# Seven products with fewer additions: M1 seeded in PSUM, M5 put where C22 will be

## The chip, the cores and the metric

The kernel runs on one core of a Trainium2 chip. Its time is the device time of that core in microseconds; three runs of the kernel before took 2271.55 to 2274.96 us, median 2273.53 us. The engines are TensorE (PE, with its weight loads as PEld), VectorE (DVE), ScalarE (ACT), GpSimd (POOL) and SyncE (SP), which issues most of the transfers.

## The reference

There are 32 graphs of 512 nodes with 512 features each, `x` and `adj` of shape (32, 512, 512), all fp32. Two layers follow each other, each with a residual:

```python
# layer 0
h = maximum(layernorm(x), 0)
deg = sum(adj, -1)
agg = (adj @ h) / maximum(deg, 1e-6)
x = x + relu(concat([h, agg], 2) @ W.T)          # W: (512, 1024)
# layer 1
h = maximum(layernorm(x), 0)
q, k = split(h @ Wqk, 2);  v = h @ Wv            # Wqk: (512, 1024), Wv: (512, 512)
agg = adj @ (k * mask)
w = mask * sum(q * agg, -1) / sqrt(512)
x = x + softmax(w, over the nodes)[..., None] * v
```

## The kernel before

**What is multiplied.** With A = adj divided by its row sums, W1 and W2 the halves of W, and M = Wq Wkᵀ, the kernel computes for each graph Y = h W2ᵀ and O = h W1ᵀ + A Y (layer 0), then U = A (mask h1), T = h1 M and V = h1 Wv (layer 1). The score of a node is the sum over a row of T times U.

**How each product is made.** A 512x512 by 512x512 product is done as 2x2 blocks of 256x256 with seven block products M1 to M7 in place of eight, which costs sums of blocks before and after. The operands' sums lie in seven slots of a tile (`left_sums`, `right_sums`, L102 to L113; `LEFT` and `RIGHT` say which slot belongs to which M). The results are

```
C11 = M1 + M2          C12 = M1 + M6 + M5 + M3
C21 = M1+M6+M7 + M4    C22 = M1+M6+M7 + M5
```

`product` (L118) does this for Y, O and U, and for V of the last graph. Its inner `m` issues one M: for each pair of operands four matmul calls, in the profile 8 rows of 128x256, into one bank of PSUM (128 x 512 fp32). Y and U have one pair of operands, O has two (h with W1, A with Y), so an M of O is twice as long. The bank `pp` collects M1, then M6, M7 and M4 on top (`start` is False), `pq` collects M5 and M3, `pr` holds M2. Between them ScalarE copies what has to be kept (`copy`, L100) and `finish` lets VectorE add (`add`, L94). A matmul that writes on into a bank waits until the engine that reads the bank is done. Before M6 this is ScalarE's copy of M1, before M7 its copy of M1+M6, before M3 its copy of M5, before M4 its copy of M1+M6+M7.

T and V together (`layer1_tv`, `ptv` in the profile) are two levels deep: seven outer M, each of seven inner block products, spread over four banks; the four parts of a bank set are added by VectorE (tv<-ptv). The inner results are put together later by `recombine` (tv<-tv). The last graph, and T and V of the one before it, use `layer1_one` (`pw`), one of T and V at a time.

**The order of work.** Four phases follow each other for each graph, written out by hand: O of graph i (14 steps), T and V of graph i−1 (14 steps), U of graph i (7 steps), Y of graph i+1 (7 steps). `run` (L167) takes a phase, which yields once per step, and a `Plan`, which says what else is queued after the matmuls of each step: statistics, sums, transposes, loads and stores of other graphs. A step's order in the queues is: its matmuls, then the plan's work of that step, then the copies and adds with which `product` finishes the step. Each engine works through its queue in the order of the program (`manual_schedule`); there is no planner.

In U the plan gives VectorE `turn` of h1T (four transposes), `recombine` (seven), `dot` (four multiplications with a sum, L611), `scores`; in Y `turn` of aT (two transposes, L278), `row_sum`, `sums` of A, `weights` and seven more `recombine`.

**Buffers.** All PSUM tiles come from one pool of eight banks. `block` (L87) gives SBUF tiles of 128 x 512 from a ring of four; O uses it for C11, C12, C22 and M5, Y and U for M5 alone, since their C lie in the result's own tile (`into`, L420). The tiles of h and A in `start` come from the same ring. W1 in its seven slots is loaded again for each graph by `Stream`, in the order `ORDER`, in which O takes them.

Of the kernel before, what the change touches and what calls it, by code (L numbers as in the profile page):

```python
# [11 lines left out]
F32 = mybir.dt.float32  # L12
# [4 lines left out]
P = 128  # L17
# [5 lines left out]
def kernel(  # L23
# [32 lines left out]

    nc = tc.nc
    B, N, F = x.shape  # L60
    C = N // P
    H = F // 2
# [6 lines left out]
    big = ctx.enter_context(tc.tile_pool(name="big", bufs=1))  # L69
    small = ctx.enter_context(tc.tile_pool(name="small", bufs=2))  # L70
    dram = ctx.enter_context(tc.tile_pool(name="dram", bufs=2, space=bass.MemoryType.DRAM))
    ps_m = ctx.enter_context(tc.tile_pool(name="ps_m", bufs=8, space=bass.MemoryType.PSUM))


    LEFT = {1: 0, 2: 1, 3: 2, 4: 3, 5: 4, 6: 5, 7: 6}
# [3 lines left out]

    PLACE = {2: 0, 3: 1, 4: 2, 7: 3, 1: 4, 6: 5, 5: 6}  # L80
    AT = {p: j for j, p in PLACE.items()}
    ORDER = [1, 2, 6, 5, 7, 3, 4]

    def slots(tag, bufs, name, pool=None):
        return (pool or big).tile([P, 7, 2, H], F32, tag=tag, bufs=bufs, name=name)

    def block(name):  # L87
        return big.tile([P, 2, H], F32, tag="tmp", bufs=4, name=name)

    def mm_tile(name):  # L90
        return ps_m.tile([P, 2, H], F32, tag="m", name=name)

    def add(o, a, b, on=None):
        (on or nc.vector).tensor_tensor(o, a, b, op=ALU.add)  # L94
# [4 lines left out]
    def copy(o, i):  # L99
        nc.scalar.activation(o, i, AF.Copy)  # L100
# [14 lines left out]
    def of(t):  # L115
        return lambda i: t[:, i]

    def product(name, terms, place, finish):  # L118

        def m(k, p, first):
            n = 0
            for lt, rt in terms:
                right = rt(k)
                for rc in range(2):
                    for dk in range(2):
                        nc.tensor.matmul(  # L130
                            p[:, rc, :],
                            lt[:, LEFT[k], dk, ts(rc, P)],
                            right[:, dk, :],
                            start=first and n == 0,
                            stop=True,
                            skip_group_check=True,
                        )
                        n += 1
                yield

        pp = mm_tile(f"pp_{name}")
        yield from m(1, pp, True)
        c11 = place(0, 0)
        copy(c11, pp)
        pr = mm_tile(f"pr_{name}")
        yield from m(2, pr, True)
        finish(0, 0, c11, pr, c11)
        yield from m(6, pp, False)
        c12 = place(0, 1)
        copy(c12, pp)  # L150
        pq = mm_tile(f"pq_{name}")
        yield from m(5, pq, True)
        m5 = block(f"m5_{name}")
        copy(m5, pq)
        yield from m(7, pp, False)
        c22 = place(1, 1)
        copy(c22, pp)
        finish(1, 1, c22, m5, c22)
        yield from m(3, pq, False)
        finish(0, 1, c12, pq, c12)  # L160
        yield from m(4, pp, False)
        finish(1, 0, None, pp, None)

    def right(t):
        return lambda k: t[:, RIGHT[k]]
# [264 lines left out]

    def layer0_y(b):
        y = Y[b] = slots("yh", 1, f"y_{b}")
        return product(f"y_{b}", [(hT, right(w2R))], *into(y))

    def layer0_out(b, w1):
        def place(r, c):
# [14 lines left out]
    def layer1_tv(b):  # L451

        t = TV[b] = tv
        left = H1T[b]

        def m(k, banks, first):
            for half in ((2, 1), (3, 0)):
                for n in half:  # L460
                    if first:
                        banks[n] = mm_tile(f"ptv_{b}_{k}_{n}")
                    for i, p in enumerate(range(2 * n, min(2 * n + 2, 7))):
                        j = AT[p]
                        nc.tensor.matmul(  # L465
                            banks[n][:, :, ts(i, P)],
                            left[:, LEFT[k], LEFT_IN[j], :],
                            mvR[:, RIGHT[k], RIGHT[j], :, :],
                            start=first and i == 0,
                            stop=True,  # L470
                            skip_group_check=True,
                        )
                yield half

        def part(o, n):
            first = [0, 4, 8, 10][n] + (2 if n < 2 else 3) * (o % 2)
            return t[:, o // 2, :, first:first + min(2, 7 - 2 * n), :].rearrange("p w b f -> p w (b f)")

        def parts(k, banks, first, use):
            for half in m(k, banks, first):  # L480
                yield
                for n in half:
                    use(n, banks[n][:, :, 0:P * min(2, 7 - 2 * n)])

        def keep(o):
            return lambda n, p: copy(part(o, n), p)

        def plus(o):
            return lambda n, p: add(part(o, n), p, part(o, n))

        pp, pr, pq, m5 = {}, {}, {}, {}

        def keep5(n, p):
            m5[n] = block(f"m5_tv_{b}_{n}")[:, :, 0:P * min(2, 7 - 2 * n)]
            copy(m5[n], p)

        yield from parts(1, pp, True, keep(0))
        yield from parts(2, pr, True, plus(0))
        yield from parts(6, pp, False, keep(1))
        yield from parts(5, pq, True, keep5)  # L500
        yield from parts(7, pp, False, lambda n, p: add(part(3, n), p, m5[n]))
        yield from parts(3, pq, False, plus(1))
        yield from parts(4, pp, False, keep(2))

    def layer1_one(b, which, held=None):

        t = TV[b] = tv
        left = H1T[b]

        def m(k, banks, first):  # L510
            for n in range(2):
                if first:
                    banks[n] = mm_tile(f"pw_{which}_{b}_{k}_{n}").rearrange("p a f -> p (a f)")
                for i, p in enumerate(range(4 * n, min(4 * n + 4, 7))):
                    j = AT[p]
                    s = LEFT[k]
                    nc.tensor.matmul(  # L517
                        banks[n][:, ts(i, P)],
                        held[:, s, :] if held is not None and j == 3 else left[:, s, LEFT_IN[j], :],
                        mvR[:, RIGHT[k], RIGHT[j], which, :],  # L520
                        start=first and i == 0,
                        stop=True,
                        skip_group_check=True,
                    )
                yield n

        def part(o, n):
            rows = t[:, o // 2, which]
            if n == 0:
                return rows[:, 0:8, :].rearrange("p (n c i) f -> p n c i f", n=2, c=2)[:, :, o % 2]  # L530
            return rows[:, 8 + 3 * (o % 2):11 + 3 * (o % 2), :]

        def like(n, p):
            if n == 0:
                return p.rearrange("p (n i f) -> p n i f", n=2, i=2)
            return p[:, 0:3 * P].rearrange("p (i f) -> p i f", f=P)

        def parts(k, banks, first, use):
            for n in m(k, banks, first):
                yield  # L540
                use(n, like(n, banks[n]))

        def keep(o):
            return lambda n, p: copy(part(o, n), p)

        def plus(o):
            return lambda n, p: add(part(o, n), p, part(o, n))

        pp, pr, pq, m5 = {}, {}, {}, {}

        def keep5(n, p):
            m5[n] = like(n, block(f"m5_w_{which}_{b}_{n}").rearrange("p a f -> p (a f)"))
            copy(m5[n], p)

        yield from parts(1, pp, True, keep(0))
        yield from parts(2, pr, True, plus(0))
        yield from parts(6, pp, False, keep(1))
        yield from parts(5, pq, True, keep5)
        yield from parts(7, pp, False, lambda n, p: add(part(3, n), p, m5[n]))
        yield from parts(3, pq, False, plus(1))  # L560
        yield from parts(4, pp, False, keep(2))

# [16 lines left out]
    class Post:  # L579
# [71 lines left out]
        def finish(self, r, c):  # L651

            v = self.blocks[r, c]
            for a in range(2):
                o = self.o[:, 2 * r + a, ts(c, H)]
                nc.vector.scalar_tensor_tensor(
                    o, v[:, a, :], self.sm[:, 2 * r + a:2 * r + a + 1], o, op0=ALU.mult, op1=ALU.add
                )
# [88 lines left out]
    def start():  # L747
# [42 lines left out]
            for k in range(2):  # L790
                turn_right(s2[h], h, k, w2R)
        for c in range(C):
            v = block(f"h_{c}").rearrange("p a f -> p (a f)")
            nc.scalar.activation(
                in_order(v), natural(X[0][:, c, :]), AF.Relu, scale=t[1][:, c:c + 1], bias=t[2][:, c:c + 1]
            )
            turn_chunk(v, c, "h")
# [7 lines left out]
        rows = {}  # L805

        def scale_a(c):
            rows[c] = block(f"a_{c}").rearrange("p a f -> p (a f)")
            nc.scalar.activation(
                in_order(rows[c]), natural(fa.n[c // 2][:, c % 2, :]), AF.Copy, scale=fa.rdeg[:, c:c + 1]  # L810
            )
# [395 lines left out]
```

## Time and profile before

| | before |
|---|---|
| median time | 2273.53 us |
| TensorE busy | 2259.1 us, 99% |
| VectorE busy | 1923.6 us, 85%, 3803 instructions |
| ScalarE busy | 1025.6 us, 45%, 1896 instructions |
| GpSimd busy | 174.8 us, 8% |
| granted TensorE clock | 0.999 |

A row of the order of time gives the start and the length of a merged group in us, the engine, the line, the operation with output and inputs by their names in the program, the shape, the number of instructions, and in brackets how long the engine sat idle before it and what ended that. Consecutive instructions on one engine overlap in the records by some 0.08 us on VectorE and 0.16 us on TensorE, so the distance between starts, not the length, is what one costs in a row: 8 matmul rows of an M are 1.89 us long, and the next M starts 1.73 us after. The lines of helpers stand for all their uses: L130 is every matmul of `product`, L94 every addition on VectorE, L97 every subtraction, L100 every ScalarE copy; the names of the tiles tell them apart.

### The profile page before, as it was taken

What the parts mean: (1) busy time and instruction counts of PE and PEld (TensorE: products, weight loads), DVE (VectorE), ACT (ScalarE), POOL (GpSimd) and SP (SyncE); (2) the same over time, 40 slices, a digit from 0 to 9 for tenths busy, and PEclk for the clock granted to TensorE, in tenths of its full rate; (3) what the DMA queues carried; (4) which work ended last, traced back from release to release, by engine and by line L of the source; (5) the groups of instructions that cost most, each with busy time, mean ns of one, the idle gap of its engine ahead of it and who ended that gap; (6) DMA issues with size and microseconds to landing.
All of it is one profiled execution on the core that took longest, in us unless ns stands there. A gap on an engine that the chain in (4) does not pass through costs nothing.

```text
span 2271.4 us, 32927 instructions
## 1 busy us (share of the span) xinstructions
PE 2259.1 (99%) x10550; PEld 1978.7 (87%) x10550; DVE 1923.6 (85%) x3803; ACT 1025.6 (45%) x1896; POOL 174.8 (8%) x260
## 2 busy tenths in 40 slices
PE   9999999999999999999999999999999999999998
PEld 7788888888888888888888888888888888888897
DVE  7798888888888888888888888888888888888778
ACT  4454443445434554444454344544444543445323
POOL 0000010000100000100000000000000010000000
PEclk9999999999999999999999999999999999999999
DMA  9978787887878777777878888777888787878543
GB/s 222 233 214 246 204 212 193 205 230 206 210 199 202 213 220 207 208 191 207 227 210 205 199 201 218 218 207 202 196 210 225 209 209 193 205 219 217 154 123 96
DMA packets 409773, 463.68 MB, mean 204 GB/s; under 512 B 37729, under 2 KB 271713, under 8 KB 405377
## 3 DMA queue, kind: packets, MB, share of 16 engines
q1 hardware_dynamic: 400192, 428.56, 69.5%
q0 software_dynamic: 8928, 32.51, 8.7%
q8 instruction: 83, 1.36, 0.3%
q14 instruction: 90, 0.73, 0.1%
q10 hardware_dynamic: 480, 0.52, 0.1%
HBM read 293.93 MB, written 167.51 MB: 203 GB/s over the span
## 4 chain that ended last, share of the span: by engine, by line
PE 93%; DMA 3%; DVE 2%; SPq 1%; ACT 0%; issue 0%; DVEq 0%; POOLq 0%; ACTq 0%
PE ptv L465 28%; PE pp_o L130 18%; PE pp_u L130 9%; PE pq_o L130 9%; PE pp_y L130 9%; PE pq_u L130 5%; PE pr_o L130 5%; PE pq_y L130 5%; PE pr_u L130 2%; PE pr_y L130 2%; PE pw L517 1%; DMA a<-in_adj_dram 1%; SPq L212 0%; DVE tv L94 0%; DMA room<-in_L_gnn_Wqk_dram 0%; DVE mv L97 0%
## 5 line engine op out<-in xcount | busy, mean ns | idle before, releaser
L465 PE MATMUL ptv<-mv,h1T 128*128 128x256 f32 x2940 | 639.7, 379 | 0.1
L465 PEld LDWEIGHTS ptv<-mv,h1T 128*128 128x128 f32 x2940 | 558.5, 190 | 76.4 <-DVE xu L444 0.5
L94 DVE TENSOR_TENSOR tv<-tv 128x256 f32<-128x256 f32 (+1 forms) x658 | 326.4, 508 | 13.4 <-ACT tv L100 1.5
L100 ACT ACTIVATE tv<-ptv 128x512 f32<-128x512 f32 (+1 forms) x360 | 184.9, 541 | 262.9 <-PE ptv L465 262.0
L130 PE MATMUL pp_y<-wide 128*128 128x256 f32 x1024 | 242.1, 379 | 1.5 <-ACT y L100 1.2
L130 PE MATMUL pp_u<-h1m,aT 128*128 128x256 f32 x1024 | 242.0, 379 | 0.0
L130 PE MATMUL pp_o<-y,aT 128*128 128x256 f32 x1024 | 241.9, 379 | 0.0
L130 PE MATMUL pp_o<-w,wide 128*128 128x256 f32 x992 | 234.3, 379 | 0.0
L130 PEld LDWEIGHTS pp_y<-wide 128*128 128x128 f32 x1024 | 194.2, 190 | 28.5 <-ACT y L100 1.6
L130 PEld LDWEIGHTS pp_u<-h1m,aT 128*128 128x128 f32 x1024 | 194.4, 190 | 27.0 <-issue 0.7
L130 PEld LDWEIGHTS pp_o<-y,aT 128*128 128x128 f32 x1024 | 194.5, 190 | 26.4
L130 PEld LDWEIGHTS pp_o<-w,wide 128*128 128x128 f32 x992 | 188.5, 190 | 25.6
L100 ACT ACTIVATE o<-pp_o 128x512 f32<-128x512 f32 x96 | 57.2, 596 | 296.0 <-PE pp_o L130 296.0
L100 ACT ACTIVATE y<-pp_y 128x512 f32<-128x512 f32 x128 | 76.3, 596 | 234.5 <-PE pp_y L130 233.4
L94 DVE TENSOR_TENSOR tv<-ptv,tv 128x512 f32<-128x512 f32 x240 | 139.6, 613 | 43.7 <-PE ptv L465 38.4
L97 DVE TENSOR_TENSOR h1T<-h1T 128x512 f32<-128x512 f32 (+2 forms) x193 | 165.8, 873 | 1.2
L100 ACT ACTIVATE xu<-pp_u 128x512 f32<-128x512 f32 x128 | 76.4, 597 | 195.9 <-PE pp_u L130 195.9
L246 POOL TENSOR_TENSOR rstd<-rstd,mhalf 128x2 f32<-128x2 f32 (+1 forms) x96 | 78.7, 820 | 651.0 <-DVE rstd L245 651.0
L130 PE MATMUL pq_y<-wide 128*128 128x256 f32 x512 | 121.0, 379 | 0.0
L130 PE MATMUL pq_o<-y,aT 128*128 128x256 f32 x512 | 121.0, 379 | 0.0
L130 PE MATMUL pq_u<-h1m,aT 128*128 128x256 f32 x512 | 121.0, 379 | 0.0
L94 DVE TENSOR_TENSOR tv<-ptv,m_tv 128x512 f32<-128x512 f32 (+1 forms) x120 | 72.0, 622 | 55.6 <-PE ptv L465 55.1
(130 smaller groups left out, 3269.4 us busy)
## 6 DMA issues: line engine op xcount, KB each, us to landing
w<-dw SPq DMA_DIRECT2D x217, 256.0 KB, 4.3
xu<-in_x_dram SPq DMA_DIRECT2D x128, 256.0 KB, 5.3
a<-in_adj_dram SPq DMA_DIRECT2D x256, 128.0 KB, 3.0
dh1T<-h1m SPq DMA_DIRECT2D x128, 256.0 KB, 3.1
dx<-xu SPq DMA_DIRECT2D x32, 1024.0 KB, 5.1
sh1T<-dh1T SPq DMA_DIRECT2D x256, 128.0 KB, 3.3
shT<-dhT SPq DMA_DIRECT2D x248, 128.0 KB, 6.0
daT<-a SPq DMA_DIRECT2D x124, 256.0 KB, 3.0
```

The source lines that it names most:

```text
L94: (on or nc.vector).tensor_tensor(o, a, b, op=ALU.add)
L97: (on or nc.vector).tensor_tensor(o, a, b, op=ALU.subtract)
L100: nc.scalar.activation(o, i, AF.Copy)
L130: nc.tensor.matmul(p[:, rc, :], lt[:, LEFT[k], dk, ts(rc, P)], right[:, dk, :], start=first and n == 0, stop=True, skip_group_check=True,)
L246: nc.gpsimd.tensor_tensor(rstd[:, a:b], rstd[:, a:b], mhalf[:, a:b], op=ALU.pow)
L465: nc.tensor.matmul(banks[n][:, :, ts(i, P)], left[:, LEFT[k], LEFT_IN[j], :], mvR[:, RIGHT[k], RIGHT[j], :, :], start=first and i == 0, st ...
L517: nc.tensor.matmul(banks[n][:, ts(i, P)], held[:, s, :] if held is not None and j == 3 else left[:, s, LEFT_IN[j], :], mvR[:, RIGHT[k], RI ...
```

## The change

The order of the block products in `product` becomes M1, M5, M6, M2, M7, M3, M4, and fewer of the additions after them are left to VectorE.

- ScalarE copies M1 from `pp` into another bank of PSUM, `pr`, and M2's matmuls then accumulate there (no `start`), so that C11 = M1 + M2 is finished by TensorE. ScalarE copies it out (Y, U), or the last operation of O reads it in PSUM. A bank of its own (`ps_r`) is kept for this; the seven others stay in the pool. The first Y does it without the seed (`seed=b > 0`), and M2 and M5 of T and V use that bank for the part that fills it.
- M5 is copied by ScalarE to the place of C22, and VectorE adds M1+M6+M7 to it from `pp`. Before, ScalarE copied M1+M6+M7 to C22 as well, and VectorE added the tile of M5.
- In T and V M5 likewise goes to its part of `tv`, and VectorE adds the rest from PSUM.
- The ring of `block` has two tiles in place of four; h and A of the first graph use `tv`, which is free then.

It is for fewer instructions on VectorE and for less SBUF. The diff, cut to its core (`layer1_one` has the same edit as `layer1_tv`):

```diff
-    ps_m = ctx.enter_context(tc.tile_pool(name="ps_m", bufs=8, space=bass.MemoryType.PSUM))
+    ps_m = ctx.enter_context(tc.tile_pool(name="ps_m", bufs=7, space=bass.MemoryType.PSUM))
+    ps_r = ctx.enter_context(tc.tile_pool(name="ps_r", bufs=1, space=bass.MemoryType.PSUM))
...
-    ORDER = [1, 2, 6, 5, 7, 3, 4]
+    ORDER = [1, 5, 6, 2, 7, 3, 4]
...
-        return big.tile([P, 2, H], F32, tag="tmp", bufs=4, name=name)
+        return big.tile([P, 2, H], F32, tag="tmp", bufs=2, name=name)
...
+    def seed_tile(name):
+        return ps_r.tile([P, 2, H], F32, tag="r", name=name)
...
-    def product(name, terms, place, finish):
+    def product(name, terms, place, finish, seed=True):
...
         pp = mm_tile(f"pp_{name}")
         yield from m(1, pp, True)
-        c11 = place(0, 0)
+        pr = seed_tile(f"pr_{name}")
+        c11 = pr if seed else place(0, 0)
         copy(c11, pp)
-        pr = mm_tile(f"pr_{name}")
-        yield from m(2, pr, True)
-        finish(0, 0, c11, pr, c11)
+        pq = mm_tile(f"pq_{name}")
+        yield from m(5, pq, True)
+        c22 = place(1, 1)
+        copy(c22, pq)
         yield from m(6, pp, False)
         c12 = place(0, 1)
         copy(c12, pp)
-        pq = mm_tile(f"pq_{name}")
-        yield from m(5, pq, True)
-        m5 = block(f"m5_{name}")
-        copy(m5, pq)
+        yield from m(2, pr, not seed)
+        if seed:
+            finish(0, 0, None, pr, None)
+        else:
+            finish(0, 0, c11, pr, c11)
         yield from m(7, pp, False)
-        c22 = place(1, 1)
-        copy(c22, pp)
-        finish(1, 1, c22, m5, c22)
+        finish(1, 1, c22, pp, c22)
         yield from m(3, pq, False)
         finish(0, 1, c12, pq, c12)
         yield from m(4, pp, False)
...
-        return product(f"y_{b}", [(hT, right(w2R))], *into(y))
+        return product(f"y_{b}", [(hT, right(w2R))], *into(y), seed=b > 0)
...
-                        banks[n] = mm_tile(f"ptv_{b}_{k}_{n}")
+                        banks[n] = (seed_tile if n == 0 and k != 1 else mm_tile)(f"ptv_{b}_{k}_{n}")
...
-        yield from parts(5, pq, True, keep5)
-        yield from parts(7, pp, False, lambda n, p: add(part(3, n), p, m5[n]))
+        yield from parts(5, pq, True, keep(3))
+        yield from parts(7, pp, False, plus(3))
...
-            v = block(f"h_{c}").rearrange("p a f -> p (a f)")
+            v = tv[:, c // 2, 0, 4 * (c % 2):4 * (c % 2) + 4, :].rearrange("p i f -> p (i f)")
...
-            rows[c] = block(f"a_{c}").rearrange("p a f -> p (a f)")
+            rows[c] = tv[:, c // 2, 1, 4 * (c % 2):4 * (c % 2) + 4, :].rearrange("p i f -> p (i f)")
```

## The prediction

> **What bounds the kernel now.** I read the page's busy shares and chain first, then what TensorE waited for, then the busy time of a long stretch, then the order of time around one graph, and last the form-by-form groups for prices.
>
> ```profile
> PE 2259.1 (99%) x10550; PEld 1978.7 (87%) x10550; DVE 1923.6 (85%) x3803; ACT 1025.6 (45%) x1896; POOL 174.8 (8%) x260
> ...
> PE 93%; DMA 3%; DVE 2%; SPq 1%; ACT 0%; issue 0%; DVEq 0%; POOLq 0%; ACTq 0%
> ```
>
> ```profile
> 189.00:1579.00 1390.00, 1390.00 (x6442) 1223.71 (x6441) 1190.64 (x2367) 639.32 (x1183) 109.84 (x160) 1.00 0.80 209
> ```
>
> ```profile
> PE spare L781 <- DVE late L753: 1.5, 1, 1.5
> PE pp_y L130 <- ACT y L100: 1.2, 1, 1.2
> PE pw L517 <- DVE tv L94: 0.8, 1, 0.8
> PE pp_y L130 <- DVE wide L97: 0.3, 1, 0.3
> ```
>
> The chain runs through TensorE. The second fence is twenty graphs of 69.50 us: TensorE (first "busy") is busy in 1390.00 of 1390.00 us. The third is all it ever waits: under 4 us in a run of 2271. The matmuls don't change, so there is almost nothing to win; the question is whether the change puts a wait where there is none. VectorE, 1190.64 of 1390.00 us, comes next.
>
> Graph 15's U, first TensorE, then VectorE:
>
> ```profile
> 1120.74 1.89 PE L130 MATMUL pp_u<-h1m,aT 128*128 128x256 f32 x8
> 1122.47 1.89 PE L130 MATMUL pq_u<-h1m,aT 128*128 128x256 f32 x8
> 1124.19 1.89 PE L130 MATMUL pp_u<-h1m,aT 128*128 128x256 f32 x8
> ```
>
> ```profile
> 1109.27 2.44 DVE L94 TENSOR_TENSOR tv<-ptv,tv 128x512 f32<-128x512 f32 x4
> 1111.62 2.01 DVE L97 TENSOR_TENSOR h1m<-h1m 128x512 f32<-128x512 f32 x3
> ...
> 1120.74 0.68 DVE L94 TENSOR_TENSOR xu<-pr_u,xu 128x512 f32<-128x512 f32 x1
> 1121.34 1.21 DVE L94 TENSOR_TENSOR tv<-tv 128x256 f32<-128x256 f32 x3
> 1122.47 0.69 DVE L611 SCALAR_TENSOR_TENSOR tv<-tv,xu 128x512 f32<-128x512 f32 x1
> ...
> 1124.91 0.69 DVE L94 TENSOR_TENSOR xu<-m_u,xu 128x512 f32<-128x512 f32 x1
> ```
>
> The three TensorE rows are M7, M3 and M4, 1.727 us apart. VectorE's last row is the C22 add of the same product: it starts 0.72 us after M4 has started and ends (1124.91 + 0.69) 1.41 us after. So VectorE runs late here, and today nobody minds: M4 waits only for ScalarE's copy of M1+M6+M7 (1122.67 to 1123.27).
>
> [...] M7 of the second Y waited 1.2 us for ScalarE's read of its bank. [...] the rows above stand in program order, so an add waits for all that is queued ahead. [...] 684 ns for xu<-m_u (both in SBUF), 680 for xu<-pq_u. [...]
>
> ```profile
> 2225.15 0.69 DVE L94 TENSOR_TENSOR tv<-pw,m_w 128x512 f32<-128x512 f32 x1
> ...
> 2225.89 1.83 PE L517 MATMUL pw<-mv,h1T 128*128 128x128 f32 x14 [0.75 <-DVE tv L94]
> ```
>
> The add ends at 2225.84, TensorE goes on 0.05 us later. These 14 take 1.83 us, where 12 elsewhere in the tail take 1.50 and two more 0.22: the restart adds another 0.1 us. M7 of the second Y (89.86 to 91.69, 1.83 instead of 1.73) shows the same 0.1. So a wait costs its end plus 0.15 us.
>
> **The change, part by part.**
>
> *Removed.* One VectorE add per product (c11 += pr), 96 of them over Y, U and O. Back to back such an add takes 0.60 us (1120.74 to 1121.34), 58 us of VectorE in all; none of it is on the path of TensorE by itself. In O also one ScalarE copy (0.60), in Y and U none (five copies before, five after).
>
> *The seed in PSUM.* ScalarE writes M1 into PSUM. No row shows such a write; a copy to SBUF takes 0.60 us[...]. I take 0.60, between the 0.4 of a half-size copy and a doubled 1.2. M6 waits for it 1.73 us after M1 ends, M2 later still; today's copy of M1 has the same 1.73 us (1115.76 to 1116.36, M6 at 1117.29). Even doubled it is hidden: 0.
>
> *Order 1, 5, 6, 2.* M5 needs its sums one place earlier. In U they are made on VectorE by 1109.4, M5 comes at 1115.6; in O the first sum of Y ends at 1140.7, it is needed at 1143.2. 0, but for the first Y: its M5 needs a left sum that ends at 18.86, where M2 ran at 18.01. M6 waited until 20.22 anyhow, so +0.5.
>
> *The smaller rings.* Two blocks serve O, which now needs two. Seven PSUM banks and the seed bank: banks come back in the same order as with eight. Hidden behind the M-stages of 1.7 to 3.5 us: 0.
>
> *C22 by VectorE from PSUM.* This is the part that counts. Four waits of TensorE for a bank (M6, M7, M3, M4) were all on ScalarE; now M4 waits for VectorE's add c22 += pp. Ahead of that add stands everything that the plan gave VectorE up to then. On M4 wait all later matmuls.
>
> - U. VectorE's work is pinned to TensorE at the last of the four tv adds: M3 of T and V gives its last result at 1113.83 − 3.02 + 0.16 = 1110.97, and that add starts at 1111.03. From there VectorE has no gap up to the C22 add. One add (0.60) goes out of this row, the rest stands. The C22 add would end at 1125.60 − 0.60 = 1125.00, M4 goes on as if started at 1125.15, against 1124.19: 0.96 us lost. The next T and V, where VectorE waits for TensorE again (1.48 us at 1105.90), wipes the slate, so it comes again with each graph. I read the same 1.41 in graphs 3 to 29 (1.50 in one), 1.94 in 2, 1.14 in 30. Thirty graphs (1 to 30): 29 × 0.96 + 0.69 = 28.5 us.
> - Y. Today the add ends 1.28 us after M4 starts. But the row ahead of it (two transposes from 1130.25 up to the add at 1136.88, 6.6 us) stands behind the add of pr_y, which waited 2.71 us for TensorE and is gone. The transposes need U's M4 to end (1126.1) and their DMA (issued by 1122.3, 3.3 us to land); the row's reduction needs ScalarE's exponential (1128.69). They can be through by 1134.2, M7 ends at 1134.7, the add at about 1135.5, M4 comes at 1136.28: no wait, 0.8 us to spare.
> - O. The add ends 1.61 us before M4 and its work gets lighter: 0.
>
> *Start.* First Y: the add ended 1.43 us after M4; with the 0.15 and the 0.5 already spent, 1.1 more, 1.6 together, of which some 1.3 lasts (the next stages wait for DMA). First U: two transposes waited 2.69 and 3.62 us for DMA, and the C22 add ended at 86.07, M4 stood at 79.89: 86.07 − 0.58 + 0.15 − 79.89 = 5.8. The second Y then no longer waits for ScalarE: −1.3. Third Y: 5.33 us late, again after DMA waits (2.40, 1.46). TensorE will be 6.7 later there, the transfers perhaps 3: 5.33 + 0.15 + 3 − 6.7 = 1.8, between 0 and 5.5. Sum 7.6.
>
> *Tail.* The last U waits too (1.86 − 0.60 + 0.15 = 1.4), and V's M4 waits for an add that today ends 2.2 us after it starts. But the end hangs on VectorE's row there, which is 0.6 shorter: −0.6 ± 1.
>
> Sum: 28.5 + 7.6 − 0.6 = 35.5; 2273.5 + 35.5 = 2309.0 us.
>
> **Rivals.**
>
> 1. *The wait is hidden:* VectorE, 58 us lighter, comes on time in U. For: 85% busy would be 82%. Against: the row in U starts from TensorE, not from old debts, and only one of the removed adds lies in it; it would need 1.6 us. Then only the start is left: some 2273 to 2280.
> 2. *Faster:* the start's waits of 1.2 and 0.3 us go, the tail is shorter, and no add is late: 2271. Against: the first U's add, pinned to DMA.
> 3. *Y waits as well*, should the transposes not move up (DMA under another timing): 1.28 − 0.60 + 0.15 = 0.83 × 29 = 24 more, 2333.
> 4. *U doesn't get its 0.60 back* (a row ahead becomes a wait): 1.41 + 0.15 = 1.56 × 30 = 47 in place of 28.5: 2327.
>
> **How the numbers follow.** One wait in each U, 0.74; rival 3, 0.11; rival 4, 0.06; rival 1, 0.05 (half of it inside 0.2%, which is 4.5 us); rival 2, 0.04, mostly within 0.2%. My own case spans 29 × 0.80 (no restart cost) to 29 × 1.15, start 3 to 11, tail −1.6 to +1.4: 2298 to 2318. With rival 4 the range is 2298 to 2328. Faster 0.03, same 0.05, slower 0.92.
>
> **What would show it.** TensorE's list of waits gains a row pp_u on VectorE's xu, some 30 times about 0.8 to 1 us, and one of 5 to 6 us; no such row for pp_o, few for pp_y. A graph takes 70.45 us in place of 69.50. VectorE has 96 adds less. The transposes of aT start right after U's M4. I am wrong if pp_u has no wait on VectorE, if pp_y has as many, if the seed copy takes over 1.5 us, or if a matmul takes longer than 216 ns.

## The result, and the profile after

The changed kernel takes 2315.16 us (median of four runs, 2313.35 to 2315.99) against 2273.93 us for the kernel before: a ratio of 1.0182, 95% interval 1.0164 to 1.0199. It is 41 us slower with 96 VectorE instructions less.

From the page: the busy shares, and the chain by engine.

```profile
PE 2272.7 (98%) x10550; PEld 1979.8 (86%) x10550; DVE 1879.1 (81%) x3707; ACT 1005.8 (43%) x1862; POOL 176.1 (8%) x260
...
PE 77%; DVE 18%; DMA 2%; issue 2%; SPq 1%; ACT 0%; DVEq 0%; POOLq 0%; POOL 0%
```

VectorE has 44.5 us less to do and is now 18% of the chain, where it was 2%. The waits of TensorE that are new and long (us in total, times, longest):

```profile
PE pp_u L136 <- DVE xu L100: 24.4, 32, 2.8
PE pp_y L136 <- DVE y L100: 3.8, 2, 2.8
PE pp_o L136 <- DVE o L100: 2.0, 1, 2.0
PE pp_v L136 <- DVE v L100: 1.6, 1, 1.6
```

Each of the 32 U now waits for VectorE, Y twice, O once, and so does the V of the last graph. Graph 15's U, TensorE and then VectorE in order of time:

```profile
1146.88 1.89 PE L136 MATMUL pp_u<-h1m,aT 128*128 128x256 f32 x8
1148.61 1.89 PE L136 MATMUL pq_u<-h1m,aT 128*128 128x256 f32 x8
1151.20 1.99 PE L136 MATMUL pp_u<-h1m,aT 128*128 128x256 f32 x8 [0.70 <-DVE xu L100]
1153.03 1.89 PE L136 MATMUL pp_y<-wide 128*128 128x256 f32 x8
```

```profile
1149.85 0.69 DVE L610 SCALAR_TENSOR_TENSOR tv<-tv,xu 128x512 f32<-128x512 f32 x1
1150.46 0.08 DVE L610 DVE_READ_ACCUMULATOR tv<-tv,xu 128x1 f32 x1
1150.46 0.68 DVE L100 TENSOR_TENSOR xu<-pp_u,xu 128x512 f32<-128x512 f32 x1
```

M4 starts 2.59 us after M3 in place of 1.73, 0.06 us after the C22 add has ended (1150.46 + 0.68), and Y follows 1.83 us later in place of 1.73: 0.86 + 0.10 = 0.96 us lost, the add itself sitting behind the fourth dot product without a gap. From U of graph 2 to U of graph 29 it is 223.91 to 2126.51, 27 graphs of 70.47 us.

### The profile page after: what moved, and what is told of

Its sections match the earlier page's. It is cut to its first block, busy times and chain, and to the rows that moved or that the text cites. A ratio compares the mean times of both kernels' runs of the same rounds, so it can differ in the third digit from the quotient of the medians.

```text
span 2314.2 us, 32911 instructions
## 1 busy us (share of the span) xinstructions
PE 2272.7 (98%) x10550; PEld 1979.8 (86%) x10550; DVE 1879.1 (81%) x3707; ACT 1005.8 (43%) x1862; POOL 176.1 (8%) x260
## 4 chain that ended last, share of the span: by engine, by line
PE 77%; DVE 18%; DMA 2%; issue 2%; SPq 1%; ACT 0%; DVEq 0%; POOLq 0%; POOL 0%
PE ptv L472 24%; PE pp_o L136 19%; PE pq_o L136 9%; PE pp_y L136 9%; DVE tv L100 8%; PE pr_o L136 5%; PE pq_y L136 4%; DVE h1T L290 3%; PE pp_u L136 3%; DVE tv L610 3%; DVE h1m L103 2%; PE pr_y L136 2%; PE pw L520 1%; DVE xu L100 1%; DMA w<-dw 0%
## 5 line engine op out<-in xcount | busy, mean ns | idle before, releaser
L106 ACT ACTIVATE tv<-ptv 128x512 f32<-128x512 f32 x480 | 241.1, 546 | 378.9 <-PE ptv L472 378.0
L100 DVE TENSOR_TENSOR tv<-ptv,tv 128x512 f32<-128x512 f32 (+1 forms) x360 | 212.0, 616 | 102.7 <-PE ptv L472 97.5
L136 PE MATMUL pp_u<-h1m,aT 128*128 128x256 f32 x1024 | 245.7, 383 | 24.4 <-DVE xu L100 24.4
L263 ACT ACTIVATE n<-n,nmr,rstd 128x512 f32<-128x512 f32 x120 | 88.2, 802 | 121.5 <-DVE nmr L257 88.9
L106 ACT ACTIVATE xu<-pp_u 128x512 f32<-128x512 f32 x64 | 38.2, 597 | 193.2 <-PE pp_u L136 193.2
L136 PE MATMUL pq_o<-w,wide 128*128 128x256 f32 x496 | 117.2, 379 | 0.0
L106 ACT ACTIVATE y<-pp_y 128x512 f32<-128x512 f32 x65 | 38.8, 597 | 178.5 <-PE pp_y L136 178.5
```

The lines of the kernel that those rows point to most:

```text
L136: nc.tensor.matmul(p[:, rc, :], lt[:, LEFT[k], dk, ts(rc, P)], right[:, dk, :], start=first and n == 0, stop=True, skip_group_check=True,)
L263: nc.scalar.activation(o, i, AF.Relu, scale=t[1][:, c:c + 1], bias=t[2][:, c:c + 1])
```

## The experiments

The theory: since M4 waits for VectorE's C22 add, it waits for all that stands ahead of that add in VectorE's queue; this is a 1 us wait in each U and a few longer ones at the start and the end. The rivals: the seed in PSUM or the bank kept for it costs TensorE; or the read of PSUM by VectorE does.

**The seed alone.** `product` with the seed and the new order, C22 as before (T and V stay as changed, the ring of blocks has four tiles; the edit is shown in short, the run has a flag for it):

```diff
+        c22 = block(f"m5_{name}")
-        c22 = place(1, 1)
         copy(c22, pq)
...
         yield from m(7, pp, False)
-        finish(1, 1, c22, pp, c22)
+        m5, c22 = c22, place(1, 1)
+        copy(c22, pp)
+        finish(1, 1, c22, m5, c22)
```

> The changed kernel with C22 made as in the kernel before in all products: M5 goes to a block of its own, ScalarE copies M1+M6+M7 to C22, VectorE adds M5 from SBUF (the ring of blocks has four tiles again). Seed in PSUM, order 1, 5, 6, 2 and the 7+1 banks stay. My theory (the loss is M4's wait for VectorE's C22 add in U, and the same wait in the first graphs and in V): M4 waits for ScalarE again, no pp_u wait on VectorE, 2272 to 2276 us, as the kernel before. Rival (the seed in PSUM, the M2 that waits for it, or the bank kept for it costs TensorE time): stays at 2300 or more.

Measured: 2274.1 us, ratio 1.0004 (0.9996 to 1.0013). The whole loss is gone. The seed, M2 on top of it, the order and the seven-and-one banks cost nothing that can be told from the total; the list of waits does have an O that waits 1.5 us for the sums of Y and a U that waits 1.1 us for those of h1, both on VectorE.

**M5 in C22 alone, no seed.** VectorE adds M2 to C11 again, in M2's new place, and the ring of blocks has four tiles for it:

```diff
     def product(name, terms, place, finish, seed=True):
+        seed = False
```

> The other half alone: M5 to the place of C22 and VectorE adds from PSUM, but no seed anywhere; VectorE adds M2 to C11 from pr as before, after M2 in its new place (four blocks). My theory: one more add of 0.60 us stands ahead of the C22 add in U, so that M4 of pp_u waits 1.57 us in place of 0.97: 30 x 0.60 = 18 us more than the changed kernel, about 2333 us. Rival (the seed is what costs): 2275 to 2285.

Measured: 2370.84 us, ratio 1.043 (1.0414 to 1.0445), 38 us more than I said. The waits:

```profile
PE pp_u L137 <- DVE xu L100: 44.5, 32, 4.5
PE pp_y L137 <- DVE y L100: 31.2, 32, 3.0
```

U is as expected: M4 starts 1.46 us late and restarts with 0.1 more, 1.57. But Y waits as well, in every graph. One of these Y on VectorE, with the end of the wait on TensorE below:

```profile
1328.77 1.38 DVE L100 TENSOR_TENSOR tv<-tv 128x512 f32<-128x512 f32 x2
1331.73 0.69 DVE L100 TENSOR_TENSOR y<-pr_y,y 128x512 f32<-128x512 f32 x1 [1.58 <-PE pr_y L137]
...
1335.32 0.68 DVE L100 TENSOR_TENSOR y<-pp_y,y 128x512 f32<-128x512 f32 x1
```

```profile
1333.25 1.89 PE L137 MATMUL pq_y<-wide 128*128 128x256 f32 x8
1336.05 1.99 PE L137 MATMUL pp_y<-wide 128*128 128x256 f32 x8 [0.91 <-DVE y L100]
```

The add of pr_y stands at the head of VectorE's queue and waits 1.58 us for M2, now the fourth product. Only then come 3 us of other work, and then the add that M4 waits for: 1.07 + 0.10 = 1.17 us. I had counted the 0.60 us of such an add, and in U only; that in Y it waits itself, and holds up what stands behind it, I had left out.

**The same with the seed in Y only,** to see whether that is it (but for the first Y):

```diff
-        seed = False
+        seed = seed and name.startswith("y_")
```

> The M5 part alone took 2371 us: besides the 1.57 us in U it showed a wait of 1.18 us in each Y. My theory for that: in Y the add of pr waits for M2, which now comes fourth, and holds up what is queued behind it on VectorE, the C22 add last. The same kernel with the seed in Y only (no add of pr in Y; U, O and V without the seed): Y's wait goes, U's 1.57 stays: 2371 - 30 x 1.18 = 2336 us. Rival (Y's wait comes from VectorE's larger total of work or from a start shifted by U's wait): 2360 or more.

Measured: 2332.37 us, ratio 1.0266 (1.0251 to 1.0282). Waits of pp_y on VectorE: 2 in place of 32; those of pp_u stay at 44.8 us in 32. So the seed in Y is worth 38 us here: it takes an add out of VectorE's queue that waited 1.58 us for TensorE and took 0.60 us itself. Both kernels have four tiles in the ring of blocks, and TensorE waits in the first graphs all the same (4.7 us in the first U of this one), so the ring of two is not what those waits need.

**The dot products behind the C22 add.** The changed kernel, with the plan of U edited:

```diff
-                    p.at(3 + c // 2, post.dot, c)
-                p.at(5, post.scores)
-                p.at(5, post.maximum)
+                    p.at(5, post.dot, c)
+                p.at(6, post.scores)
+                p.at(6, post.maximum)
```

> The changed kernel with one edit in the plan of U: the four dot products of VectorE come after the matmuls of M3 and so behind the C22 add in its queue (scores and maximum one step later). My theory: the C22 add can end 2.44 us earlier, then it waits for M7 and ends 0.8 us before M4 starts; the thirty waits of 0.97 us are gone, those of the first graphs and of the last stay: 2315 - 28 = 2287 us. Rival (the wait comes from the read of the bank or the add's own length, not from what is queued ahead of it): within 3 us of 2315.

Measured: 2289.74 us, ratio 1.0072 (1.0057 to 1.0087). The same work in another order takes 25 us off, where 28 were expected; its four runs lie up to 7 us apart, and the profiled one is the fastest (2285.71). A graph's U, VectorE, then TensorE, then the busy time of TensorE (first "busy") over 25 graphs:

```profile
1133.82 0.69 DVE L100 TENSOR_TENSOR xu<-pp_u,xu 128x512 f32<-128x512 f32 x1 [0.78 <-PE pp_u L136]
1134.42 0.68 DVE L610 SCALAR_TENSOR_TENSOR tv<-tv,xu 128x512 f32<-128x512 f32 x1
```

```profile
1133.54 1.89 PE L136 MATMUL pq_u<-h1m,aT 128*128 128x256 f32 x8
1135.27 1.89 PE L136 MATMUL pp_u<-h1m,aT 128*128 128x256 f32 x8
```

```profile
260.00:2000.00 1740.00, 1740.00 (x8064) 1531.73 (x8063) 1451.50 (x2877) 783.45 (x1453) 140.45 (x201) 1.00 0.80 208
```

The add now waits 0.78 us for M7 and ends 0.76 us before M4. It still reads PSUM and still takes 0.69 us, so neither is what cost. TensorE is busy 1740.00 of 1740.00 us; all that is left lies in the first three graphs and the tail.

**The first graphs and the end repaired too.** Dots as above, and the older way to C22 (a flag `by_act`, the edit of the first experiment) where the other waits were (only the arguments are shown):

```diff
+    by_act=b < 3                  # Y, O
+    by_act=b < 3 or b == B - 1    # U
+    by_act=True                   # V
```

> The dot products later as in the run before it, and C22 by way of ScalarE as in the kernel before where the first and last waits were: Y, O and U of graphs 0 to 2, U of the last graph and V (four blocks). My theory: all added waits are gone and the end of V is a little shorter: 2270 to 2275 us, the same as the kernel before; a kernel that keeps 85 fewer VectorE adds without loss. Rival (something else in the start costs, such as the order with M5 second): 2278 to 2285.

Measured: 2273.74 us, ratio 1.0002 (0.9993 to 1.0011). The loss is gone again, and VectorE still has 96 instructions less than in the kernel before. Of the new waits the list keeps one of 1.7 us in O of graph 2 and one of 0.7 us in the first Y.

**And the old order where M5 second made TensorE wait** (Y and O of graph 0, O of graph 2, these without a seed):

```diff
+    old=b == 0          # Y
+    old=b in (0, 2)     # O; W1 of graph 2 is streamed in the old order
```

> The repaired kernel of the first four runs (dot products later, ScalarE's way to C22 in the first three graphs, the last U and V), with the old order of the products and no seed in Y and O of graph 0 and in O of graph 2, where M5 in second place made TensorE wait (1.7 us in O of graph 2, 0.7 in the first Y). My theory: those waits go, 1.5 to 2.5 us less than the repaired kernel: about 2271.5 us, 0.1% under the kernel before. Rival (the end is set elsewhere in the start, by transfers): no difference, 2273.5.

Measured: 2271.81 us, ratio 0.9998 (0.9990 to 1.0006). The two waits are gone from the list, but the time can't be told from the kernel before, nor, as the two intervals overlap, from the repaired kernel: the 1.5 to 2.5 us that I expected are not shown. No version here beats the kernel before: in its long stretch TensorE is busy all the time, and what is left lies in the head and the tail.

**Longer waits.** The trace after the change had one thing that no sum of waits explains. Granted TensorE clock (third number from the end) in five stretches: right after the 2.8 us wait of the first U, the 3.4 us after that, after the wait in the third Y, after the one in O of graph 2, and after V's:

```profile
84.20:85.60 1.40, 1.40 (x6) 1.24 (x7) 1.33 (x4) 0.00 (x0) 0.26 (x1) 0.99 1.25 209
85.60:89.00 3.40, 3.40 (x9) 2.66 (x8) 2.78 (x5) 0.60 (x1) 0.92 (x2) 0.50 1.11 216
171.20:174.40 3.20, 3.13 (x8) 2.55 (x9) 3.13 (x7) 0.00 (x0) 0.48 (x1) 0.51 0.16 55
198.30:201.70 3.40, 3.40 (x10) 2.72 (x9) 3.30 (x6) 2.92 (x4) 0.00 (x0) 0.51 0.50 181
2304.00:2308.00 4.00, 1.99 (x8) 1.44 (x8) 3.93 (x9) 0.00 (x0) 0.00 (x0) 1.00 0.35 91
```

After three of these waits, all but V's, the clock is halved for some 3.4 us, and matmuls start 0.43 us apart in place of 0.22. By their starts that cost 1.68, 1.49 and 1.68 us, 4.85 in all. To see how long a wait must be, two or three idle VectorE operations more went ahead of the C22 add in U of graphs 3 to 29:

```diff
+                for k in range(3 if 2 < i < 30 else 0):
+                    p.at(4, lambda: sub(idle, hT[:, 0], hT[:, 1]))
```

> The changed kernel with two more VectorE subtractions (128x512 in SBUF, into a tile nobody reads) ahead of the C22 add in U of graphs 3 to 29. Each delays the add by 0.60 us. If a wait costs its own length: 27 x 1.20 = 32 us more, 2348 us, with a wait of 2.2 us in U. If TensorE runs at half its rate for some 3 us after a wait that is long enough (seen after the waits of 2.2 to 3 us in the first graphs, not after 1.8 us in V): up to 27 x 1.6 = 43 us more, 2391.

> The same with three more subtractions. If a wait costs its own length: 27 x 1.80 = 49 us more, 2364 us, with a wait of 2.8 us. With the half rate after each wait: 43 us on top, some 2407.

Measured: 2355.01 us with two, 2395.73 with three (1.0365 and 1.0544). By the distance of starts, TensorE stood still for 2.19 us in U with two and 2.92 with three, where it was 0.86; each operation cost 0.67 to 0.69. In the lists the pp_u waits are 61.1 and 80.7 us in 32, in place of 24.4. Of the 27 waits of 2.19 us three were followed by the half clock (mean granted clock of the run 0.995), of those of 2.92 us fourteen, nearly every second one (0.986). Take two that follow each other, with three operations. One ends at 676.93 and is followed by the half clock, the next ends at 751.14 and is not:

```profile
674.00:677.74 3.74, 0.99 (x5) 0.73 (x5) 3.64 (x9) 0.00 (x0) 0.38 (x1) 1.00 0.91 270
677.74:681.15 3.41, 3.41 (x10) 2.70 (x9) 1.30 (x2) 0.60 (x1) 0.00 (x0) 0.50 0.86 242
681.15:684.56 3.41, 3.41 (x18) 3.00 (x17) 1.39 (x3) 1.24 (x3) 0.39 (x1) 1.00 1.06 209
749.42:752.83 3.41, 1.69 (x8) 1.51 (x9) 2.61 (x7) 0.00 (x0) 0.38 (x1) 1.00 0.96 246
752.83:756.24 3.41, 3.41 (x18) 3.00 (x17) 1.69 (x3) 1.38 (x3) 0.14 (x1) 1.00 1.01 221
```

The difference is where the wait lies. In the trace after the change the three half-clock stretches ahead of the last matmul begin at 85.57, 170.90 and 198.21, 25 and 8 times 3.413 us apart, and each is 3.41 us long. The 3.41 us ahead of each:

```profile
82.15:85.56 3.41, 1.36 (x6) 1.24 (x7) 3.27 (x9) 0.00 (x0) 0.22 (x1) 1.00 1.24 204
167.49:170.90 3.41, 0.94 (x5) 0.49 (x3) 3.31 (x8) 0.00 (x0) 0.00 (x0) 1.00 1.02 340
194.79:198.20 3.41, 1.37 (x7) 0.89 (x6) 3.12 (x9) 0.00 (x0) 1.06 (x1) 1.00 1.06 313
```

TensorE was idle there for 2.05, 2.47 and 2.04 us. In the run with three operations the half clock begins at 677.74. Of the wait that ended at 676.93, 2.61 us lay in the 3.413 us ahead of that (674.33 to 677.74); of the one that ended at 751.14, in steps of 3.413 us counted from 677.74, 1.72 us lay in one (from 749.42, 21 steps on) and 1.20 in the one before. So of these five waits the four that had 2.04 us or more in one step were followed by the half clock, and the one that was divided into 1.20 and 1.72 was not. That the other waits of these runs divide in the same way is not shown here.

With 1.6 us for each half clock, and the first graphs taken as they were, the sums close within 3 us: 2315 + 27 × 1.33 + 3 × 1.6 = 2356, and 2315 + 27 × 2.06 + 14 × 1.6 = 2393. Neither of the two cases expected for each run held: the half clock comes after some of the waits, not after all or none, and an operation cost 0.67 to 0.69 us in place of 0.60.

## Why the prediction was right, step by step

The wait in U is the one that was forecast, and it makes up two thirds of the loss. The start, though, fell outside its own range of 3 to 11 us, and its terms missed both ways.

- *The bound, and one wait per U.* Right, and to the hundredth in graph 15: 0.96 us forecast, 0.96 measured. From U of graph 1 to that of 30 TensorE fell 28.5 us behind, as worked out (0.70, 0.96, 27 times 0.97, 0.70). Graph 1 was luck: the prediction counted 0.96 there too without having read the row, where the add ended 3.42 us after M4's start (153.96 + 0.68 against 151.22), by its own rule 2.97 us. It lost 0.70 because TensorE was 4.3 us late by then and the add only 1.4.
- *A wait costs its end plus 0.15 us.* Right: the restart took 0.06 + 0.10. What a long wait costs beside, half the clock (1.49 to 1.68 us in this trace), is not in this rule.
- *The seed copy and the smaller rings at nothing.* Right: ScalarE's copy into PSUM took 582 ns, 597 into SBUF. The seed alone gave the time of the kernel before. VectorE's busy time fell by 44.5 us, not the 58 counted for 96 adds; no term of the sum hangs on it, and why it is less is not shown.
- *The order.* Nearly right: the 0.5 us in the first Y came, as a wait of 0.7; in O of graph 2 M5 second made TensorE wait 1.7 us once the other waits were gone (the repaired kernel), which I hadn't seen.
- *No wait in Y.* Right. The first of graph 15's two transposes starts at 1153.23, when U's M4 is done (Y's first matmul starts at 1153.03), and the C22 add of Y waits 0.40 us for M7 and not the other way round. That the add of pr_y had to go is shown too: without the seed in Y the wait is there (1.17 us), though not in the way of rival 3, as the transposes start right after U's M4 in that kernel as well (1324.82) and the add holds up the queue behind them.
- *O without a wait.* Right but for graph 2, where TensorE waits 2.0 us.
- *The start, 7.6 us.* This is the term that was mis-sized: 12.85 us. The lag behind the kernel before, gained in each phase, and what of it the half clock took, in us:

  | phase | forecast | measured | of it half clock |
  |---|---|---|---|
  | first Y | 1.3 | 1.65 | 0 |
  | first U | 5.8 | 3.1 | 0.4 |
  | second Y | −1.3 | −0.2 | 1.2 |
  | third Y | 1.8 | 4.6 | 1.5 |
  | O of graph 2 | 0 | 4.0 | 1.7 |
  | the rest | 0 | −0.3 | 0 |
  | sum | 7.6 | 12.85 | 4.85 |

  The kernel before has no half clock until its last matmul has ended, so no row of it shows this cost. Without the half clock the sum would be 8.0, but that is in part luck: in the first U a wait of 5 to 6 us was forecast and one of 2.9 came, because the forecast set the add against M4's old place, 79.89, though TensorE was already 1.4 us late there, and because the last transposes started 1.3 us earlier than before (79.76 in place of 81.10). Third Y and O of graph 2 waited 1.3 and 2.3 us longer than forecast, which makes up for it. In O of graph 2 VectorE stood before the C22 add waiting for the rows of a later x:

```profile
189.84 0.69 DVE L247 BATCH_NORM_STATS2 st<-n 128x6 f32<-128x512 f32 x1 [5.71 <-DMA n<-in_x_dram]
...
194.94 0.69 DVE L247 BATCH_NORM_STATS2 st<-n 128x6 f32<-128x512 f32 x1 [2.71 <-DMA n<-in_x_dram]
...
196.76 0.69 DVE L100 TENSOR_TENSOR o<-pp_o,o 128x512 f32<-128x512 f32 x1
```

  I had taken it that what TensorE loses earlier gives VectorE room. But these loads stand in SyncE's queue behind loads of W1, whose buffers TensorE has to free: they were issued at 180.33 and 183.80 in place of 170.78 and 174.25, 9.6 us later, just as far as TensorE itself had fallen behind by then (9.56), and VectorE could go on some 10 us after that. In the kernel before VectorE came late enough by itself (the first of these rows at 182.81) not to wait for them.
- *The tail, −0.6.* Wrong: +1.4 measured, the very end of the bounds. The last U's wait (1.42, as worked out) did reach the end, which was not expected.
- *The rivals.* 1 and 2 are out: U's wait is there. 3 is out, as Y waits twice and not in each graph. 4 is out for this kernel; its number, 1.56 us in U, is what U shows when the add of pr is put back (1.57).

The sum was 35.5 us, the profiled span grew by 42.8: 28.5 + 12.85 + 1.4.

## What to carry to other kernels

Where TensorE is busy all the time, as here (1390.00 of 1390.00 us before), instructions saved elsewhere were worth nothing (96 fewer in the repaired kernel, the same time), and what counts of an edit is which engine each bank is now handed back by, and what stands in that engine's queue ahead of the instruction that hands it back. How late such an instruction runs can be read in the trace of the kernel before, also while nobody waits for it; move it ahead of work that has time, as the dot products here, before making anybody wait for it. An instruction that itself waits, put into a queue, costs its successors the wait and not just its length (1.58 us and 0.60 for the add of pr_y). How late it is says what it costs only together with how late TensorE is by then: in the first graphs, where the two moved against each other, the forecast missed.

## What the runs showed of the hardware

A wait of TensorE can cost more than itself when it is long. After the change, waits of 2.8, 2.8 and 2.0 us (first U, third Y, O of graph 2) were followed by 3.41 us at a granted clock of 0.50, which cost another 1.49 to 1.68 us each; V's of 1.6 us and the 27 of 0.70 in U were not. With stand-stills of 2.19 us it came after 3 of 27 (more_2, mean granted clock 0.995), with 2.92 us after 14 of 27 (more_3, 0.986). The place of the wait counted as well: where 2.04 to 2.61 us of one step of 3.413 us were idle the half clock came (three waits after the change, one of more_3), and where 2.92 us were divided into 1.20 and 1.72 it did not (one of more_3).

VectorE's add of 128x512 took 684 ns with an operand in PSUM (xu<-pp_u, after) as with both in SBUF (xu<-m_u, before), and ScalarE's copy of a bank 582 ns into PSUM (pr_u<-pp_u), 597 into SBUF (xu<-pp_u).
